# Attention times a gated network in float32: values projected for four heads at once, with fewer buffers

## The chip, the core and the metric

The kernel runs as one launch on one core of a Trainium2 chip. The metric is device time in microseconds (us); lower is better. All inputs and the output are float32 in DRAM.

## The reference

For x of shape [4, 512, 512], with 16 heads of width 128 and an inner width of 1408:

```
xn = layernorm(x)                                   # over the last axis, eps 1e-5
q, k, v = xn W_Q[h] + b_Q[h], xn W_K[h] + b_K[h], xn W_V[h] + b_V[h]
attn = softmax(where(causal, q k^T / sqrt(128), -1e5))
s = sum over h of (attn v) W_O[h] + b_O
f = (silu((xn gate_w^T) gate_s) * ((xn up_w^T) up_s)) down_w^T * down_s
out = x + s * silu(f)
```

## The kernel before

Float32 products go through TensorE as passes of float32r: a tile is held as `hi + lo` (class `Split`), and `mm3` (L90) issues three matmuls for each product, of hi·lo, hi·hi and lo·hi. Making a split costs one copy on ScalarE (`hi`) and one subtraction on VectorE (`lo`); weights are split by ScalarE and GpSimd (`split_w`, L133). The engines work in parallel, each in the order of its own queue, and that order is the order in which the program is written (`manual_schedule`); nothing reorders it.

The attention part is a loop of 64 steps n, over `heads` = (g, b, i): a group g of two heads (HG = 2, so 8 groups), the sequence b (0 to 3), and the head i in the group (0 or 1). A group is 8 steps. One step works on three heads at once:

- `softmax` (L272): scores of this step's head in three PSUM tiles `sc`, four fused mask-and-minimum passes on VectorE (L298), four exponentials on ScalarE (L312), four reciprocals on VectorE (L315), four scalings on GpSimd (L316). It leaves the probabilities in `p`, in one SBUF buffer.
- `turn_p` (L319): turns the probabilities for the value product. Six transposes of 32x32 squares on VectorE write `sq` (L330); a DMA on the queue of SyncE (SP) writes `sq` to DRAM as `turn` (L335); when that has landed, four DMAs on the same queue read `turn` back as `ptr` (L341).
- `split_p` (L346): splits the turned `ptr` of the *previous* step's head into `pt`, two halves, each a ScalarE copy (`pth`, L357) and a VectorE subtraction (`ptl`, L358).
- `project` (L241) makes q and then k of the *next* step's head; their `hi` leaves PSUM on ScalarE (L252), their `lo` on VectorE (L255).
- `attend` (L376), through `attend_last`: the value product z of the previous step's head, from `pt` and the values. It goes key tile by key tile, three passes each.

Two more pieces of work fill the step. In steps with i = 0, `project_v` (L232) makes the values of group g for sequence b, four tiles of 128 tokens by 256 columns (two heads), two before q and two after z. In steps with i = 1, `project_out` (L397) adds the pair of heads of the preceding sequence (`prev`) to the output projection: four tiles, two before q and two after z; each loads its sum so far from DRAM on ScalarE's queue (`load_acc`, L390), adds on VectorE (L406) and stores on SP's queue (L407). `look` (L434) is one VectorE pass per step over a tile of the second part's weights, in steps 9 to 41. Loads of the next group's weights are issued on ScalarE's queue (`prepare_qk`, `prepare_v`, `prepare_o`), and `split_pending` splits them in the step in which they are due.

The order of `split_p` against `turn_p` in a step is set by one flag. With `early` true (steps 2, 3 and the last), the previous head's `split_p` comes after `softmax` and ahead of `turn_p`; in all other steps it comes after `turn_p`, and then two heads' `ptr` are alive at once, for which `ptr` has two buffers:

```
early = n < HG * HG or nxt is None
...
if n > 1 and early:
    pt = split_p(raw)
look()
fill(range(0, half))
if nxt is not None:
    raw_next = turn_p(of)
if not early:
    pt = split_p(raw)
```

The second part, the gated network (`ffn`, L624 on), is not touched by the change but for the name of one constant.

Of the kernel before, what the change touches and what calls it, by code (L numbers as in the profile page):

```python
# [10 lines left out]
F32 = mybir.dt.float32  # L11
# [8 lines left out]
HG = 2  # L20
IGNORE = -100000.0
# [3 lines left out]
LOW_BITS = (1 << 12) - 1  # of a float32's significand, beyond float32r's  # L25


class Split:
    """A float32 tile as hi + lo, each of float32r's 12 significant bits (exact)."""
# [13 lines left out]
def kernel(  # L43
    ctx: ExitStack,
    tc: tile.TileContext,
    x: bass.AP,        # [B, S, D]
    w_q: bass.AP,      # [H, P, ND, E]    w_q[h, p, c, e] = W_Q[h, c*P + p, e]
    w_k: bass.AP,      # [H, P, ND, E]
    w_v: bass.AP,      # [H/HG, P, ND, HG*E]
    w_o: bass.AP,      # [H, E, D]  # L50
    consts: bass.AP,   # [P, 3 H + 2 NF]  b_q, b_k, b_v by head, gate_s, up_s by chunk
    b_o: bass.AP,      # [1, D]
    gate_w: bass.AP,   # [NF, P, ND, P]   gate_w[f, p, c, i] = W[f*P + i, c*P + p]
    up_w: bass.AP,     # [NF, P, ND, P]
    down_w: bass.AP,   # [NF, P, D]       transposed
    down_s: bass.AP,   # [1, D]
    out: bass.AP,      # [B, S, D]
):
    """x + attention(ln(x)) * silu(ffn(ln(x))), in float32.

    A float32 product a*b goes through the tensor engine as three passes of
    float32r: with a = ah + al and b = bh + bl exactly (12 bits each), the passes
    carry ah*bh, ah*bl and al*bh; al*bl is below float32's own rounding.
    """
# [19 lines left out]
    ]  # L84
    acc_d = [
# [4 lines left out]
    def mm3(ps, a, b, first, last):  # L90
        nc.tensor.matmul(ps, a.hi, b.lo, start=first, stop=False)  # L91
        nc.tensor.matmul(ps, a.hi, b.hi, start=False, stop=False)  # L92
        nc.tensor.matmul(ps, a.lo, b.hi, start=False, stop=last)  # L93

# [1 line left out]
    with ExitStack() as at:  # L96
# [6 lines left out]
        vp = at.enter_context(tc.tile_pool(name="vp", bufs=2 * NT))  # L103
# [46 lines left out]
        def split_pending(n):  # L150
            """Split the weights that are due by step n."""
            for due, dst, raw in [p for p in pending if p[0] <= n]:
                split_w(dst, raw)
            pending[:] = [p for p in pending if p[0] > n]

        def prepare(due, dst, src, name):
            """Load a [P, D] piece of a weight; split_pending() splits it when it is due."""
            pending.append((due, dst, stage(src, name)))
# [6 lines left out]
        def prepare_v(g, due):  # L165
            wv[g] = weight(wvop, [P, ND, HG * E], f"wv{g}", "wv")
            half = ND // 2
            for i in range(2):
                c = slice(i * half, (i + 1) * half)
                src = w_v[g][:, c, :].rearrange("p c e -> p (c e)")  # L170
                prepare(due, flat(wv[g][:, c, :]), src, f"wvr{g}_{i}")
# [10 lines left out]
        def ln_stats(b, tt):  # L182
            """Means and variances of some of b's tiles."""
# [14 lines left out]
        def table(func):  # L198
            """Have ScalarE load the function's table now."""
            nc.scalar.activation(small.tile([P, 1], F32, name="junk"), eps, func)  # L200

        def warm_up():
            """Matmuls from the start on, for TensorE's clock."""
# [4 lines left out]
        def ln_normalize(b, t):  # L208
# [4 lines left out]
            xn = lnp.tile([P, D], F32, name="xn")  # L213
            nc.vector.tensor_scalar(xn, xt, mv[:, 0:1], rstd, ALU.subtract, ALU.mult)
            xn_of[b, t] = xn
# [16 lines left out]
        def project_v(g, b, t):  # L232
            ps = ps_mm.tile([P, HG * E], F32, name="psv", tag="mm")
            for c in range(ND):
                mm3(ps, xnT[b][:, c, ts(t, P)], wv[g][:, c, :], c == 0, c == ND - 1)
            v = weight(vp, [P, HG * E], f"v{g}_{b}_{t}", "v")
            nc.scalar.copy(v.hi, ps)
            nc.vector.tensor_tensor(v.lo, ps, v.hi32, ALU.subtract)
            v_of.setdefault((g, b), []).append(v)

        def project(b, h, w, bias, name, parts=1):  # L241
            """q or k of a head, [E, S], by parts; yields before each one leaves PSUM."""
# [18 lines left out]
        # The causal half of the scores is kept by query tile t: [P queries, keys up  # L261
        # to its diagonal], that of the transposed probabilities by key tile j: [P keys,
        # queries from its diagonal on], these in the order [quarter, slot, Q] where
        # slot(j, t) counts the pairs and a query is t * P + quarter * Q + its column.
# [7 lines left out]
        def softmax(qT, kT):  # L272
# [3 lines left out]
            for pack in PACK:  # L276
# [3 lines left out]
                for t in pack:  # L280
                    n = (t + 1) * P
                    where[t] = sc[:, at_ : at_ + n]
                    if t > 0:
                        mm3(where[t], qT[:, ts(t, P)], kT[:, :n], True, True)
                    at_ += n
                if 0 in pack:
                    # so few columns that q.hi's two passes go as one, side by side
# [31 lines left out]
        def turn_p(of):  # L319
            """Transpose the probabilities: squares of Q on VectorE, which DMA puts in place."""  # L320
# [18 lines left out]
            raw = pp.tile([P, NQ, NS * Q], F32, name="ptr", tag="ptr", bufs=2)  # L339
# [21 lines left out]
        def transpose_p(of):  # L361
            """The same on TensorE, in less time."""
# [13 lines left out]
        def attend(h, pt, vs):  # L376
            z = ps_mm.tile([P, NT, P], F32, name="z", tag="mm")
            for j in range(NT):
                c = slice(slot[j], slot[j] + NT - j)
                mm3(z[:, j:, :], vs[j][:, ts(h % HG, E)], pt[:, c, :], j == 0, j == NT - 1)  # L380
            zT = weight(zp, [P, NT, P], f"z{h}", "z")
            # the rows of the probabilities sum to one, so v's bias goes in here
# [14 lines left out]
        def project_out(g, b, t, zTs):  # L397
# [3 lines left out]
            if g == 0:  # L401
                a = ap.tile([P, D], F32, name="a", tag="a")
                nc.vector.tensor_tensor(a, ps, bo_bc, ALU.add)
# [14 lines left out]
        # Are all the ffn's weights float32r already (12 significant bits)?  The  # L418
        # bits of each partition are or-ed together on the way.
# [19 lines left out]
        def low_bits():  # L439
            """By partition, the low 12 bits found; 0 if they are clear in every weight."""  # L440
# [5 lines left out]
        def any_of(low):  # L446
            """Their sum as [1, 1] int32."""
# [6 lines left out]
        with tc.manual_schedule():  # L454
# [4 lines left out]
            prepare_v(0, -2)  # L459
# [45 lines left out]
            bo_bc = load_const(b_o.broadcast_to([P, D]), [P, D], "bo_bc")  # L505
            ds_bc = load_const(down_s.broadcast_to([P, D]), [P, D], "ds_bc")
# [11 lines left out]
            for n, (g, b, i) in enumerate(heads):  # L518
# [4 lines left out]
                # the layernorm of a later b, from its statistics to its transposing  # L523
# [7 lines left out]
                def fill(ks):  # L531
                    for t in ks:
                        if i == 0 and not (n == 0 and t == 0):
                            project_v(g, b, t)
                        if i == HG - 1 and prev is not None:
                            project_out(*prev, t, zs[prev])

                # at the ends there is less to do while the last step's p is turned
                early = n < HG * HG or nxt is None
# [3 lines left out]
                if n > 1 and early:  # L543
                    pt = split_p(raw)
                look()
                half = NT // 2 if nxt is not None else NT - 1
                fill(range(0, half))
                if nxt is not None:
                    raw_next = turn_p(of)
                if not early:  # L550
                    pt = split_p(raw)
                split_pending(n)
                # loads for the steps to come
# [4 lines left out]
                if nxt is None:  # L558
                    # in wv's place, which is done with
# [7 lines left out]
                if g + 1 < NG:  # L567
                    # in place of this group's, when these have had their last use
# [228 lines left out]
```

## Time and profile before

| | |
|---|---|
| runs, median (lowest to highest) | 1237.92 us (1237.6 to 1238.34) |
| profiled execution, first to last instruction (span) | 1235.7 us |
| what lies outside the span | 1.9 to 2.6 us, from the runs |
| granted TensorE clock, mean | 0.998 |
| PE busy | 1208.2 us (98%) |
| DVE / ACT / POOL busy | 828.0 / 526.2 / 302.4 us |
| DMA moved | 215.55 MB, mean 174 GB/s |
| first scores of step 0, and of step 63 | 19.88 and 968.77 us |

How to read it: the page is one profiled execution; PE is TensorE's matmuls, PEld its weight loads, DVE VectorE, ACT ScalarE, POOL GpSimd, SPq and ACTq the DMA queues of SyncE and ScalarE. A matmul's duration includes its way through the array, so that two neighbours overlap: what a matmul costs in a row of them is the distance from its start to the next one's. A line of the timeline has start and duration in us, engine, source line, operation, output and inputs, the count of merged instructions, and in brackets the engine's idle time before it and what ended that. A line of the waits has the total in us, the number of waits and the longest. A DMA row ends with the median time from issue to landing.

### The profile page before, as it was taken

What the parts mean: (1) busy time and instruction counts of PE and PEld (TensorE: products, weight loads), DVE (VectorE), ACT (ScalarE), POOL (GpSimd) and SP (SyncE); (2) the same over time, 40 slices, a digit from 0 to 9 for tenths busy, and PEclk for the clock granted to TensorE, in tenths of its full rate; (3) what the DMA queues carried; (4) which work ended last, traced back from release to release, by engine and by line L of the source; (5) the groups of instructions that cost most, each with busy time, mean ns of one, the idle gap of its engine ahead of it and who ended that gap; (6) DMA issues with size and microseconds to landing.
All of it is one profiled execution on the core that took longest, in us unless ns stands there. A gap on an engine that the chain in (4) does not pass through costs nothing.

```text
span 1235.7 us, 18827 instructions
## 1 busy us (share of the span) xinstructions
PE 1208.2 (98%) x6514; PEld 1049.4 (85%) x6514; DVE 828.0 (67%) x2044; ACT 526.2 (43%) x1169; POOL 302.4 (24%) x433
## 2 busy tenths in 40 slices
PE   8999999999999999999999999999999999999997
PEld 7888888888888888888888888888888888888886
DVE  6897777777777777777777676767676634334343
ACT  5654444444444444444544454445444332323231
POOL 4212321232123212321322141214121341212110
PEclk9999999999999999999999999999999999999999
DMA  4464456656665666566655555566544793637341
GB/s 163 134 191 144 137 167 192 205 171 188 188 205 170 189 203 207 172 199 198 217 176 175 179 173 171 169 188 183 170 163 153 239 331 95 205 94 206 84 145 38
DMA packets 117912, 215.55 MB, mean 174 GB/s; under 512 B 13232, under 2 KB 45744, under 8 KB 117808
## 3 DMA queue, kind: packets, MB, share of 16 engines
q1 hardware_dynamic: 74016, 134.51, 34.2%
q10 hardware_dynamic: 29376, 53.26, 14.4%
q0 software_dynamic: 14416, 26.48, 8.0%
q8 instruction: 53, 0.87, 0.3%
q14 instruction: 51, 0.42, 0.1%
HBM read 135.17 MB, written 79.04 MB: 173 GB/s over the span
## 4 chain that ended last, share of the span: by engine, by line
PE 82%; DVE 11%; ACT 2%; POOL 1%; issue 1%; DMA 1%; SPq 0%; DVEq 0%; ACTq 0%
PE pd L660 6%; PE pg L660 6%; PE pu L660 6%; DVE ptl L358 5%; PE pso L91 5%; PE psv L91 4%; PE pso L93 4%; PE pso L92 4%; PE psv L93 4%; PE psv L92 4%; PE z L91 3%; PE psq L91 3%; PE psq L92 3%; PE psq L93 3%; PE psk L93 3%; PE psk L92 3%
## 5 line engine op out<-in xcount | busy, mean ns | idle before, releaser
L316 POOL TENSOR_SCALAR p<-p,rtot 128x512 f32<-128x512 f32 (+3 forms) x256 | 148.6, 602 | 688.8 <-DVE rtot L315 688.8
L312 ACT ACTIVATE p<-p,nmax 128x512 f32<-128x512 f32 (+3 forms) x256 | 140.9, 552 | 147.1 <-DVE nmax L298 147.1
L358 DVE TENSOR_TENSOR ptl<-ptr,pth 128x640 fp32r<-128x640 f32 x126 | 132.8, 1092 | 1.4 <-ACT pth L357 1.4
L330 DVE STREAM_TRANSPOSE sq<-p 128x256 f32<-128x256 f32 x378 | 113.3, 362 | 0.0
L298 DVE CUSTOM_DVE_ANT_0 p<-sc,mask 128x512 f32<-128x512 f32 (+2 forms) x192 | 96.5, 553 | 0.3 <-PE sc L93 0.3
L252 ACT ACTIVATE k<-psk,consts 128x512 fp32r<-128x512 f32 (+1 forms) x65 | 44.2, 680 | 108.3 <-PE psk L93 108.1
L357 ACT CAST pth<-ptr 128x640 fp32r<-128x640 f32 x126 | 84.9, 724 | 1.5 <-DMA ptr<-turn 1.5
L252 ACT ACTIVATE q<-psq,consts 128x512 fp32r<-128x512 f32 (+1 forms) x65 | 44.3, 682 | 96.8 <-PE psq L93 72.4
L406 DVE TENSOR_TENSOR a<-pso,a 128x512 f32<-128x512 f32 x108 | 72.1, 687 | 17.4 <-PE pso L93 17.4
L255 DVE SCALAR_TENSOR_TENSOR k<-psk,consts,k 128x512 fp32r<-128x512 f32 (+1 forms) x65 | 48.0, 739 | 53.2 <-ACT k L252 53.1
L686 DVE SCALAR_TENSOR_TENSOR hd<-pu,consts,sg 128x512 f32<-128x512 f32 x44 | 33.0, 751 | 66.7 <-PE pu L660 62.2
L315 DVE RECIPROCAL rtot<-tot 128x1 f32<-128x1 f32 x256 | 41.6, 163 | 42.7 <-ACT p L312 36.3
L91 PE MATMUL sc<-k,q 128*128 128x512 f32 (+2 forms) x192 | 65.8, 342 | 1.8 <-DVE xl L225 1.6
L92 PE MATMUL sc<-k,q 128*128 128x512 f32 (+2 forms) x192 | 64.7, 337 | 0.0
L93 PE MATMUL sc<-k,q 128*128 128x512 f32 (+2 forms) x192 | 64.7, 337 | 0.0
L255 DVE SCALAR_TENSOR_TENSOR q<-psq,consts,q 128x512 fp32r<-128x512 f32 (+1 forms) x65 | 47.6, 732 | 7.6 <-ACT q L252 7.6
L312 ACT ACTIVATION_READ_ACCUMULATOR p<-p,nmax 128x1 f32 x256 | 47.7, 186 | 0.0
L91 PEld LDWEIGHTS sc<-k,q 128*128 128x128 f32 x192 | 36.2, 188 | 7.9 <-DVE xl L225 3.6
L716 ACT ACTIVATE o<-o 128x512 f32<-128x512 f32 (+1 forms) x17 | 10.3, 607 | 68.8 <-DVE o L715 68.8
L91 PE MATMUL z<-ptl,v_0h 128*128 128x512 f32 x64 | 27.0, 421 | 12.6 <-DVE ptl L358 12.6
L92 PEld LDWEIGHTS sc<-k,q 128*128 128x128 f32 x192 | 36.2, 188 | 3.6
L93 PEld LDWEIGHTS sc<-k,q 128*128 128x128 f32 x192 | 36.1, 188 | 2.6
(734 smaller groups left out, 3811.2 us busy)
## 6 DMA issues: line engine op xcount, KB each, us to landing
turn<-sq SPq DMA_DIRECT2D x63, 640.0 KB, 3.7
ptr<-turn SPq DMA_DIRECT2D x252, 160.0 KB, 3.4
acc<-a SPq DMA_DIRECT2D x124, 256.0 KB, 3.8
a<-acc ACTq DMA_DIRECT2D x108, 256.0 KB, 2.9
xt<-in_x SPq DMA_DIRECT2D x16, 256.0 KB, 4.2
wor<-in_w_o ACTq DMA_DIRECT2D x16, 256.0 KB, 5.1
fa<-acc SPq DMA_DIRECT2D x16, 256.0 KB, 6.3
fx<-in_x SPq DMA_DIRECT2D x16, 256.0 KB, 6.7
```

Source lines behind the costliest of these rows:

```text
L91: nc.tensor.matmul(ps, a.hi, b.lo, start=first, stop=False)
L92: nc.tensor.matmul(ps, a.hi, b.hi, start=False, stop=False)
L93: nc.tensor.matmul(ps, a.lo, b.hi, start=False, stop=last)
L252: nc.scalar.activation(q.hi[:, at_], ps[:, at_], AF.Identity, bias=bias[:, h : h + 1])
L255: nc.vector.scalar_tensor_tensor(q.lo[:, at_], ps[:, at_], bias[:, h : h + 1], q.hi32[:, at_], ALU.add, ALU.subtract,)
L298: nc.vector.tensor_tensor_reduce(out=of[t], in0=where[t], in1=add, scale=-SCALE, scalar=BIG, op0=ALU.add, op1=ALU.min, accum_out=nmax[t],)
L312: nc.scalar.activation(of[t], of[t], AF.Exp, bias=nmax[t], scale=-1.0, accum_out=tot)
L316: nc.gpsimd.tensor_scalar(of[t], of[t], rtot, 1.0, ALU.mult, ALU.mult)
L330: nc.vector.transpose(dst.rearrange("p a s i -> p s a i"), src.rearrange("p (s a i) -> p s a i", s=n, i=Q),)
L357: nc.scalar.copy(dst(pt.hi), src)
L358: nc.vector.tensor_tensor(dst(pt.lo), src, dst(pt.hi32), ALU.subtract)
L660: nc.tensor.matmul(ps, l, r, start=first and k == 0, stop=last and k == len(pairs) - 1)
```

## The change

- `project_v` computes 512 columns (four heads, VG = 2 groups) at a time, in every second group (g even). The first half of the result is used from SBUF; the second half is written to DRAM (`v_d`, 64 DMAs of 256 KB on SP's queue), and in the odd groups read back by `load_v` (32 DMAs of 512 KB on ScalarE's queue), one sequence ahead.
- The work of a step is spread anew. In even groups a step with i = 0 projects values tile 0 ahead of q and tile 1 after z, a step with i = 1 tiles 2 and 3 ahead of q. In odd groups no values are projected. Of the output projection, two tiles go after z in steps with i = 1, and the other two ahead of q in the step after (i = 0 of the next sequence, `prev2`).
- `split_p` always comes ahead of `turn_p`, as before in steps 2 and 3; `ptr` has one buffer in place of two.
- The layernorm writes in place, the two broadcast constants share a tile (`row_bc`), the value pool has 6 buffers of 512 columns hi and lo in place of 8 of 256. The weights of the values are loaded and split in four pieces of which the last two wait for a staging buffer at the start, and in two steps of an odd group later.
- `mm3` begins with hi·hi; in the scores the pass with k's `lo` comes last. `attend` goes over all key tiles with hi·hi, then with v's `lo`, then with the probabilities' `lo`, in the order 0, 3, 1, 2 of key tiles.

```diff
-        vp = at.enter_context(tc.tile_pool(name="vp", bufs=2 * NT))
+        vp = at.enter_context(tc.tile_pool(name="vp", bufs=NT + 2))
...
         def project_v(g, b, t):
-            ps = ps_mm.tile([P, HG * E], F32, name="psv", tag="mm")
+            ps = ps_mm.tile([P, VG * HG * E], F32, name="psv", tag="mm")
             for c in range(ND):
                 mm3(ps, xnT[b][:, c, ts(t, P)], wv[g][:, c, :], c == 0, c == ND - 1)
-            v = weight(vp, [P, HG * E], f"v{g}_{b}_{t}", "v")
+            both = vp.tile([P, 2, VG * HG * E], F32R, name=f"v{g}_{b}_{t}", tag="v")
+            v = Split(both[:, 0], both[:, 1])
             nc.scalar.copy(v.hi, ps)
             nc.vector.tensor_tensor(v.lo, ps, v.hi32, ALU.subtract)
-            v_of.setdefault((g, b), []).append(v)
+            v_of.setdefault((g, b), []).append(v[:, : HG * E])
+            nc.sync.dma_start(
+                out=v_d[g // VG][b][t // 2, :, t % 2], in_=both.bitcast(F32)[:, :, HG * E :]
+            )
+
+        def load_v(g, b):
+            for k in range(NT // 2):
+                two = vp.tile([P, 2, 2, HG * E], F32R, name=f"v{g}_{b}_{k}", tag="v")
+                nc.scalar.dma_start(out=two.bitcast(F32), in_=v_d[g // VG][b][k])
+                for t in range(2):
+                    v_of.setdefault((g, b), []).append(Split(two[:, t, 0], two[:, t, 1]))
...
-            raw = pp.tile([P, NQ, NS * Q], F32, name="ptr", tag="ptr", bufs=2)
+            raw = pp.tile([P, NQ, NS * Q], F32, name="ptr", tag="ptr")
...
-            for j in range(NT):
-                c = slice(slot[j], slot[j] + NT - j)
-                mm3(z[:, j:, :], vs[j][:, ts(h % HG, E)], pt[:, c, :], j == 0, j == NT - 1)
+            todo = []
+            for part, other in (("hi", "hi"), ("lo", "hi"), ("hi", "lo")):
+                for j in (0, NT - 1, 1, 2):
+                    v = getattr(vs[j], part)[:, ts(h % HG, E)]
+                    p_ = getattr(pt, other)[:, slot[j] : slot[j] + NT - j, :]
+                    todo.append((z[:, j:, :], v, p_))
+            for k, (o, v, p_) in enumerate(todo):
+                nc.tensor.matmul(o, v, p_, start=k == 0, stop=k == len(todo) - 1)
...
-                def fill(ks):
-                    for t in ks:
-                        if i == 0 and not (n == 0 and t == 0):
-                            project_v(g, b, t)
-                        if i == HG - 1 and prev is not None:
+                prev2 = divmod(gb - 2, B) if gb > 1 else None
+                values = g % VG == 0
+
+                def early():
+                    if i == 0:
+                        if prev2 is not None:
+                            for t in range(NT // 2, NT):
+                                project_out(*prev2, t, zs[prev2])
+                        if values and n > 0:
+                            project_v(g, b, 0)
+                    elif values:
+                        project_v(g, b, 2)
+                        project_v(g, b, 3)
+
+                def late():
+                    if i == 0 and values:
+                        project_v(g, b, 1)
+                    if i == HG - 1 and prev is not None:
+                        for t in range(NT // 2):
                             project_out(*prev, t, zs[prev])
...
-                if n > 1 and early:
+                if n > 1:
                     pt = split_p(raw)
                 look()
-                half = NT // 2 if nxt is not None else NT - 1
-                fill(range(0, half))
+                early()
+                if nxt is None:
+                    for t in range(NT - 1):
+                        project_out(*prev, t, zs[prev])
                 if nxt is not None:
                     raw_next = turn_p(of)
-                if not early:
-                    pt = split_p(raw)
                 split_pending(n)
...
+                    if i == HG - 1 and divmod(gb + 1, B)[0] % VG:
+                        load_v(*divmod(gb + 1, B))
+                elif i == HG - 1 and b + 1 < B:
+                    load_v(g, b + 1)
```

## The prediction, made before the changed kernel ran

> **What bounds the kernel now.** I read the page's busy times first, then the waits, then the timelines of TensorE, VectorE, ScalarE and SP's queue over single steps, and at last the DMA rows.
>
> ```profile
> PE 1208.2 (98%) x6514; PEld 1049.4 (85%) x6514; DVE 828.0 (67%) x2044; ACT 526.2 (43%) x1169; POOL 302.4 (24%) x433
> ```
>
> TensorE sets the time: 98% busy, and 27 us idle in all. Of that idle time the waits (PE's own) name one large cause, the `lo` half of the turned probabilities, which comes late to the value product:
>
> ```profile
> PE z L91 <- DVE ptl L358: 12.6, 19, 0.8
> ```
>
> The timeline of PE gives the price of a matmul, as the distance of two starts (columns: start, duration, both us):
>
> ```profile
> 300.21 0.39 PE L93 MATMUL psk<-xh,wk5l 128*128 128x512 f32 x1
> 300.44 0.39 PE L91 MATMUL psk<-xl,wk5h 128*128 128x512 f32 x1
> ...
> 304.08 0.28 PE L92 MATMUL psv<-wv2h,xh 128*128 128x256 f32 x1
> 304.20 0.28 PE L93 MATMUL psv<-wv2h,xl 128*128 128x256 f32 x1
> ```
>
> Over longer rows of them this is 0.2273 us for 512 columns (11 distances from 311.38 to 313.88) and 0.1195 us for 256 (22 from 304.08 to 306.71). So a step's parts on PE are: scores 1.75 (306.83 to 308.58), a tile of the output projection 6 x 0.2273 = 1.36, q and k 12 x 0.2273 = 2.73 each, z 1.98 (301.93 to 303.91), a value tile 12 x 0.1195 = 1.43. A step with i = 0 is then 1.75 + 4 x 1.43 + 5.46 + 1.98 = 14.92, one with i = 1 14.63; the scores of steps 8 and 63 start at 140.28 and 968.77, so that the mean step takes 15.06, 0.28 of it waits.
>
> The changed order of `split_p` and `turn_p` makes a second resource matter, the way of the probabilities through DRAM. Steps 2 and 3 of the kernel before already run in the order that the change gives to all. Step 2, ACT, DVE and SP in turn:
>
> ```profile
> 52.77 1.34 ACT L357 CAST pth<-ptr 128x640 fp32r<-128x640 f32 x2
> ```
> ```profile
> 53.51 1.64 DVE L358 TENSOR_TENSOR ptl<-ptr,pth 128x640 fp32r<-128x640 f32 x2 [0.45 <-ACT pth L357]
> 55.07 0.41 DVE L238 TENSOR_TENSOR v_0l<-psv,v_0h 128x256 fp32r<-128x256 f32 x1
> ...
> 55.74 1.79 DVE L330 STREAM_TRANSPOSE sq<-p 128x256 f32<-128x256 f32 x6
> ```
> ```profile
> 57.56 0.34 SPq L335 DMA_DIRECT2D turn<-sq  x1
> 60.58 1.73 SPq L341 DMA_DIRECT2D ptr<-turn  x4
> ```
>
> The old head's split stands on DVE ahead of the new head's transposes. In the other steps it stands behind them (step 20 of before):
>
> ```profile
> 327.07 1.80 DVE L330 STREAM_TRANSPOSE sq<-p 128x256 f32<-128x256 f32 x6
> 328.80 1.52 DVE L358 TENSOR_TENSOR ptl<-ptr,pth 128x640 fp32r<-128x640 f32 x2
> ```
>
> There a turned head has nearly two steps to come back; nothing waits for it (ScalarE waited for `ptr` 1.5 us in all). The way itself is long:
>
> ```profile
> turn<-sq SPq DMA_DIRECT2D x63, 640.0 KB, 3.7
> ptr<-turn SPq DMA_DIRECT2D x252, 160.0 KB, 3.4
> ```
>
> The four reads are issued over 1.73 us, so with these medians the last has landed 3.7 + 1.3 + 3.4 = 8.4 us after the transposes. Read step by step from the landings, this time (call it L) is 7.8 to 12.4, median 9.1. In groups 1 to 4 it is 9.35 in steps with i = 0 and 10.25 in those with i = 1, where two stores of sums stand just ahead on SP's queue; in groups 5 to 7, without the loads for `look`, 8.4 and 9.7.
>
> **The change part by part.**
>
> *Wider value projection.* 1536 matmuls of 256 columns become 768 of 512: 768 x (2 x 0.1195 - 0.2273) = 9.0 us less on PE, all of it on the path while PE sets the time. The trace's two distances put the cost that a matmul has besides its columns at 11.7 ns. The Trainium skill, page "TensorE: Matmul & The Clock Gate", Part 1 ("Wait — 56ns, not 53.3ns?"), gives a warm matmul only about 2.5 ns beside its columns; by that the saving would be 1.9 us and the time 7 us higher, an estimate from the page, which this trace does not support.
>
> *Reordered value product and scores.* The pass with the probabilities' `lo` goes last, and that `lo` is made earlier in the step, so the 12.6 us of idle go, with the stretched first passes beside them. Matmul count and columns are unchanged; a lone 128-column pass costs its successor 0.06 (308.58 to 308.87 is 0.29 for a 512-column pass), three in a row now cost 0.15 in z: no difference. What is late next on PE is only its own work: with all waits gone 56 steps lose 0.28 x 56 = 16 us.
>
> *Work spread anew.* PE's share of a step becomes 1.75 + 2 x 1.36 + 2 x 2.73 + 5.46 + 1.98 = 17.37 in even groups and 1.75 + 2.72 + 5.46 + 1.98 = 11.91 in odd ones (11.9 for i = 0 and i = 1 alike). Steps 8 to 63 were 56 x 15.06 = 843.4; on PE alone they become 24 x 17.37 + 32 x 11.91 = 798.0, 45.4 less. Group 0 gets dearer, as it does the values of group 1 too: 15 tiles in its loop from 1.43 to 2.73 (+19.5), two tiles of output projection fewer (-2.7), so +16.8.
>
> *Start.* Pieces three and four of the values' weights need staging buffers that GpSimd frees at 8.8 and 10.0 (where the second head's weights are loaded now); they land some 3.4 later, and ScalarE's queue stands at their copies: the third layernorm statistic behind them, at 10.66 now, moves to about 14.2, and the first value tile takes 1.3 more: +4.8, with 1.3 to 7 as bounds.
>
> *Split ahead of turn, one `ptr` buffer.* This is the part that decides. In every step a head's return from DRAM now stands ahead, on DVE, of the next head's transposes, and these ahead of that head's trip. This is a loop that goes round once in a step: landing, split 2.30 (52.77 to 55.07), `look` 0.74 where there is one, for i = 0 two adds 1.20, transposes 1.82 (55.74 to 57.56), then L. Behind the waiting copy `pth` on ACT stand the hi of q and k, for which the next scores wait; so when the loop is longer than PE's 11.91, PE waits. In odd groups with `look` (1 and 3), L for i = 0 is as before for i = 1, since the stores of sums now stand there, 10.25; for i = 1 I take 10.0, between 9.35 and 10.25, as 1 MB of `load_v` takes the place of the stores. Sum: 2.30 + 0.74 + 1.20 + 1.82 + 10.25 = 16.3 and 2.30 + 0.74 + 1.82 + 10.0 = 14.9, mean 15.6. In groups 5 and 7, with L of 9.4 and 9.2 (between 8.4 and 9.7): 14.7 and 13.3, mean 14.0. That is 16 x 15.6 + 16 x 14.0 = 474, and 7 more for the steps in which GpSimd splits weights beside `look` (two-input passes from SBUF take 1600 ns beside it where 797 is the rule) and for two looks in group 5: 481, or 15.0 a step, against 381 on PE: +100. In even groups the loop is 2.30 + 0.74 + 1.20 + 0.65 + 1.82 + 10.5 = 17.2 and 16.3, just under PE's 17.37; I allow +4 in all, 0 to 15.
>
> *DMA.* 64 stores and 32 loads, 33.5 MB more on 215.55: they matter through L alone. *ScalarE and VectorE* save one fixed cost per pair of value tiles (two copies of 0.37 become one of about 0.62), off the path. The in-place layernorm moves the loads of x behind PE's transposes on SP's queue, ahead of a `turn` that comes some us later; the shared constant and the value pool make no wait, since the last readers are a step old: 0, and if that cover failed, a few us once.
>
> The Trainium skill, same page and part, says that an idle window of about 3.4 us halves TensorE's clock until it has been busy for as long. That speaks against steps that leave PE idle for 3 us; the trace of before, with PE's clock at 0.99 to 1.00 in each stretch and no idle stretch over 1.7 us, cannot show it. By the page such a step would cost PE up to 1.7 us, an estimate, and that lies inside the idle time that the loop leaves.
>
> **Sum.** Against the profiled execution of 1235.7 (the runs' median is 2.2 above, and I carry that over): -45.4 + 16.8 + 4.8 + 100 + 4 = +80, so 1316 as a span and 1318 as a time.
>
> **Rivals.** (a) *PE stays the bound in odd groups too.* For it: the matmuls do become fewer, and all of PE's waits have a remedy here. Then only -45.4 + 16.8 + 4.8 = -24 remains: 1214. The point from which it decides: an odd step below 11.91 + 24/32 = 12.65 us makes the change a gain. That needs L near 7.2 on the mean, below the 7.8 that is the smallest of 63 in the trace. (b) *The loop holds, but light:* L at its quiet 7.8 to 8.4 throughout, since even groups move other data: odd steps of 12.7 to 13.5, 1240 to 1265. (c) *L grows with the added transfers* to the 12 of the slowest steps: odd steps of 17, and the even groups above PE by half a us a step: 1375 to 1390. (d) That the narrow matmuls were not the cost, and the 9.0 us do not come: 1327, inside the forecast.
>
> **How the numbers follow.** The forecast, loop-bound odd groups at 13.5 to 16.6 a step, has 0.80 (1265 to 1370); (a) 0.06; (b) 0.07, of which a quarter ends within 0.2% of before; (c) 0.07. The range runs from 1262 to 1375. A measurement of this kernel tells about 0.2% (2.5 us) from no change: faster 0.06, same 0.02, slower 0.92.
>
> **What would show it.** Right: odd groups' steps near 15, even ones near 17.4; ACT `pth` waiting for the DMA of `ptr` for some 3 us in nearly each odd step (before: 1.5 us in all), PE's idle time near 120 us, its wait for `ptl` in z gone, and 768 value matmuls 0.227 apart. Wrong: steps under 12.65 in odd groups, `pth` not waiting, or PE idle in even groups.

## The result, and the profile after

| | before | after |
|---|---|---|
| runs, median (lowest to highest) | 1238.13 us (1237.6 to 1239.83) | 1326.61 us (1324.91 to 1327.73) |
| profiled execution: span | 1235.7 us | 1325.3 us |
| first scores of step 0 | 19.88 us | 24.63 us |
| granted TensorE clock, mean | 0.998 | 0.97 |
| DMA moved | 215.55 MB | 249.01 MB |

The changed kernel is slower: 1.0711 times the time of before, with a 95% interval of 1.0696 to 1.0727. That lies 9 us above the 1318 that was forecast, and inside the range.

The busy times of the page after, its row of the granted clock, and the engines' shares of the chain that ended last:

```profile
PE 1239.3 (94%) x5746; PEld 1031.8 (78%) x5746; DVE 786.8 (59%) x1980; ACT 519.6 (39%) x1105; POOL 297.7 (22%) x433
...
PEclk8999998899999988999999989999999999999999
...
PE 56%; DMA 19%; DVE 14%; ACT 4%; SPq 3%; issue 3%; POOL 1%; ACTq 0%; DVEq 0%; POOLq 0%
```

There are 768 matmuls fewer, and yet TensorE is busy for longer than before, at 94% of a longer span. In the clock's row the 8s behind the first stand in three places, which are the odd groups 1, 3 and 5 (a slice is 33.1 us; group 1 is about 164 to 288). The chain that ends last is TensorE's work for little more than half; DMA, VectorE and the two queues hold most of the rest. Both the waits and the DMA rows say where:

```profile
DVE ptl L383 <- ACT pth L382: 177.9, 62, 7.8
ACT pth L382 <- DMA ptr<-turn: 144.8, 41, 7.3
...
PE z L412 <- ACT pth L382: 33.7, 27, 3.3
...
PE sc L98 <- ACT k L277: 22.6, 7, 3.8
```
```profile
turn<-sq SPq DMA_DIRECT2D x63, 640.0 KB, 4.6
ptr<-turn SPq DMA_DIRECT2D x252, 160.0 KB, 3.3
```

TensorE's 12.6 us of waiting for `ptl` in z are gone. In their place ScalarE's copy `pth` waits for the turned probabilities 41 times, 3.5 us each; before it did so for 1.5 us in all. TensorE then waits for that copy in z, and for k (which stands behind the copy on ScalarE) in the scores.

A cut through four groups shows the two kinds of step (columns: stretch, length, busy time and count of PE, PEld, DVE, ACT and POOL, clock, DMA share, GB/s). These are about groups 1 to 4:

```profile
164.00:288.00 124.00, 105.48 (x472) 86.93 (x472) 78.21 (x211) 50.17 (x114) 31.65 (x42) 0.92 0.65 203
288.00:428.00 140.00, 139.84 (x667) 117.99 (x666) 92.11 (x237) 57.39 (x126) 28.25 (x39) 1.00 0.66 206
428.00:554.00 126.00, 106.97 (x474) 87.64 (x473) 78.89 (x213) 50.25 (x114) 31.66 (x42) 0.91 0.68 208
554.00:694.00 140.00, 139.84 (x667) 117.96 (x666) 92.27 (x236) 57.15 (x126) 30.16 (x38) 1.00 0.64 204
```

In even groups TensorE has no gap: 139.84 of 140, at 17.4 us a step. In odd groups it has 18.5 to 19 us of gaps in eight steps, a lower clock, and no other engine is busy for more than two thirds of the time. Nothing is at its limit there, so the limit is a chain through several engines. It can be walked in step 28 (group 3), with ACT first, then SP, DVE and PE:

```profile
493.00 0.19 ACT L337 ACTIVATION_READ_ACCUMULATOR p<-p,nmax 128x1 f32 x1
499.42 0.72 ACT L382 CAST pth<-ptr 128x640 fp32r<-128x640 f32 x1 [6.24 <-DMA ptr<-turn]
...
505.60 0.69 ACT L277 ACTIVATE q<-psq,consts 128x512 fp32r<-128x512 f32 x1 [3.77 <-issue]
```
```profile
494.41 1.73 SPq L366 DMA_DIRECT2D ptr<-turn  x4
...
506.36 0.32 SPq L360 DMA_DIRECT2D turn<-sq  x1
510.85 1.74 SPq L366 DMA_DIRECT2D ptr<-turn  x4
```
```profile
500.18 1.56 DVE L383 TENSOR_TENSOR ptl<-ptr,pth 128x640 fp32r<-128x640 f32 x2 [6.80 <-ACT pth L382]
501.66 1.76 DVE L469 TENSOR_TENSOR bits<-bits,look 128x512 int32<-128x512 int32 x1
503.34 1.27 DVE L438 TENSOR_TENSOR a<-pso,a 128x512 f32<-128x512 f32 x2
504.54 1.79 DVE L355 STREAM_TRANSPOSE sq<-p 128x256 f32<-128x256 f32 x6
```
```profile
506.92 0.80 PE L98 MATMUL sc<-k,q 128*128 128x512 f32 x1 [2.79 <-ACT k L277]
```

ScalarE has finished the exponentials at 493.2 and stands still until the head of the step before has landed. The four reads were issued at 494.41; the copy starts at 499.42, 5.0 us later. Then VectorE does the `lo` half, the pass for `look`, two adds and at last the transposes of the next head, and only at 506.36 can that head's trip begin. Its reads are issued 4.5 us later, and the next round has started. From 494.41 to 510.85 it is 16.4 us, where TensorE's own work for such a step is 11.9.

Not every wait in this step is on the loop. Between the copy and q, ScalarE stands for 3.77 us at its own load issues, two of which wait for GpSimd to free a staging buffer, and the scores' wait of 2.79 us comes from that. It costs nothing here: the next step's exponentials are done at 512.0 all the same, and the copy behind them waits until 515.95 for its DMA.

### The profile page after: what moved, and what is told of

The parts are those of the page before. It is cut to its first block, busy times and chain, and to the rows that moved or that the text cites. A ratio compares the mean times of both kernels' runs of the same rounds, so it can differ in the third digit from the quotient of the medians.

```text
span 1325.3 us, 17330 instructions
## 1 busy us (share of the span) xinstructions
PE 1239.3 (94%) x5746; PEld 1031.8 (78%) x5746; DVE 786.8 (59%) x1980; ACT 519.6 (39%) x1105; POOL 297.7 (22%) x433
## 2 busy tenths in 40 slices
DMA packets 141970, 249.01 MB, mean 188 GB/s; under 512 B 14768, under 2 KB 67760, under 8 KB 141872
## 4 chain that ended last, share of the span: by engine, by line
PE 56%; DMA 19%; DVE 14%; ACT 4%; SPq 3%; issue 3%; POOL 1%; ACTq 0%; DVEq 0%; POOLq 0%
DMA turn<-sq 9%; DMA ptr<-turn 9%; PE psv L103 8%; PE pd L712 6%; PE pg L712 6%; PE pu L712 6%; PE z L412 4%; DVE sq L355 4%; PE psv L98 4%; PE pso L103 4%; PE psk L103 4%; PE psq L103 4%; DVE ptl L383 3%; PE sc L103 3%; SPq L366 3%
## 5 line engine op out<-in xcount | busy, mean ns | idle before, releaser
L341 POOL TENSOR_SCALAR p<-p,rtot 128x512 f32<-128x512 f32 (+3 forms) x256 | 154.5, 622 | 696.4 <-DVE rtot L340 696.4
L383 DVE TENSOR_TENSOR ptl<-ptr,pth 128x640 fp32r<-128x640 f32 x126 | 99.2, 827 | 177.9 <-ACT pth L382 177.9
L382 ACT CAST pth<-ptr 128x640 fp32r<-128x640 f32 x126 | 85.1, 724 | 145.1 <-DMA ptr<-turn 144.8
L412 PE MATMUL z<-pth,v 128*128 128x512 f32 (+3 forms) x512 | 98.7, 337 | 33.7 <-ACT pth L382 33.7
L412 PEld LDWEIGHTS z<-pth,v 128*128 128x128 f32 x512 | 81.8, 195 | 54.3 <-ACT pth L382 45.5
L103 PE MATMUL sc<-k,q 128*128 128x512 f32 (+2 forms) x384 | 109.8, 371 | 12.1 <-DVE q L280 10.6
L98 PE MATMUL sc<-k,q 128*128 128x512 f32 (+2 forms) x192 | 71.8, 374 | 25.3 <-ACT k L277 22.6
L103 PEld LDWEIGHTS sc<-k,q 128*128 128x128 f32 x384 | 74.0, 207 | 27.2 <-DVE q L280 13.8
L253 DVE TENSOR_TENSOR v<-psv,v 128x512 fp32r<-128x512 f32 x64 | 43.7, 685 | 39.5 <-ACT v L252 39.2
L98 PEld LDWEIGHTS sc<-k,q 128*128 128x128 f32 x192 | 39.7, 207 | 33.2 <-ACT k L277 25.2
L252 ACT CAST v<-psv 128x512 fp32r<-128x512 f32 x64 | 37.3, 583 | 71.2 <-PE psv L103 71.2
L280 DVE SCALAR_TENSOR_TENSOR q<-psq,consts,q 128x512 fp32r<-128x512 f32 (+1 forms) x65 | 46.6, 717 | 14.6 <-ACT q L277 14.5
L412 PE MATMUL z<-ptl,v 128*128 128x512 f32 (+3 forms) x256 | 54.0, 335 | 0.0
## 6 DMA issues: line engine op xcount, KB each, us to landing
v<-v ACTq DMA_DIRECT2D x32, 512.0 KB, 6.9
```

Of the source, the lines that this page charges most:

```text
L98: nc.tensor.matmul(ps, a.hi, b.hi, start=first, stop=False)
L103: nc.tensor.matmul(ps, l, r, start=False, stop=last and k == 1)
L280: nc.vector.scalar_tensor_tensor(q.lo[:, at_], ps[:, at_], bias[:, h : h + 1], q.hi32[:, at_], ALU.add, ALU.subtract,)
L341: nc.gpsimd.tensor_scalar(of[t], of[t], rtot, 1.0, ALU.mult, ALU.mult)
L382: nc.scalar.copy(dst(pt.hi), src)
L383: nc.vector.tensor_tensor(dst(pt.lo), src, dst(pt.hi32), ALU.subtract)
```

## Experiments

The kernel before was run beside each (medians 1238.07 to 1238.82). Here is the whole set; a step is the mean one of odd groups.

| run | time, us | ratio (95%) | odd step, us | `pth` waits, us (times) |
|---|---|---|---|---|
| after | 1326.61 | 1.0711 (1.0696 to 1.0727) | 15.2 | 144.8 (41) |
| e1_two_ptr | 1326.33 | 1.0709 (1.0688 to 1.0731) | 15.1 | 140.5 (42) |
| e2_late_split | 1283.47 | 1.0370 (1.0335 to 1.0404) | 13.9 | 49.7 (24) |
| e3_early_in_before | 1223.43 | 0.9878 (0.9861 to 0.9894) | 14.8 | 5.6 (8) |
| e4_more_pe | 1330.29 | 1.0741 (1.0709 to 1.0774) | 15.3 | 98.4 (35) |
| e5_no_v_traffic | 1279.00 | 1.0325 (1.0302 to 1.0348) | 13.7 | 77.7 (35) |
| e6_late_look_pool | 1265.37 | 1.0220 (1.0171 to 1.0269) | 13.4 | 66.1 (27) |
| e7_order_in_before | 1222.49 | 0.9869 (0.9853 to 0.9886) | 14.8 | 0.9 (2) |
| e8_early_and_order | 1224.22 | 0.9886 (0.9870 to 0.9903) | 14.8 | 5.2 (8) |
| e9_late_no_traffic | 1231.96 | 0.9944 (0.9921 to 0.9966) | 12.4 | 25.3 (19) |
| e10_light_steps | 1188.58 | 0.9593 (0.9565 to 0.9621) | 13.6 (groups 4 to 7) | 106.9 (40) |

### Is it the buffer? (e1_two_ptr)

The changed kernel with two buffers for `ptr`. For the room, the sums of the output projection use a pool of two, and two of the four tiles borrow the buffers of the layernorm's input.

```diff
-            raw = pp.tile([P, NQ, NS * Q], F32, name="ptr", tag="ptr")
+            raw = pp.tile([P, NQ, NS * Q], F32, name="ptr", tag="ptr", bufs=2)
```

> The changed kernel with two buffers for ptr in place of one; the order of split_p ahead of turn_p stays. (For room, two of the four tiles of sums loaded from DRAM are taken from the layernorm's pool.) Theory, the loop is made by the order of the two on VectorE's queue: no change, 1320 to 1333 us, odd groups' steps at 15.2 to 15.6, pth still waiting some 145 us in all for the DMA of ptr. Rival, the single buffer holds the reads of the next head back: odd steps fall towards PE's 11.9 to 12.6, 1215 to 1240 us.

Measured: 1326.33, the same as the changed kernel, and the same wait:

```profile
ACT pth L382 <- DMA ptr<-turn: 140.5, 42, 7.3
```

So the single buffer costs nothing. With the split ahead of the turn, one buffer is all that this order can use.

### Is it the order of split and turn? (e2_late_split, e3_early_in_before)

First, e1 with the old order from step 4 on:

```diff
-                if n > 1:
+                early_split = n < HG * HG or nxt is None
+                if n > 1 and early_split:
                     pt = split_p(raw)
...
                     raw_next = turn_p(of)
+                if not early_split:
+                    pt = split_p(raw)
```

> As e1_two_ptr, and split_p goes back behind turn_p from step 4 on, as in the kernel before; wide values, their way through DRAM, the spread over two steps and the order of the products stay. Theory, the loop: it no longer goes round once a step, so odd groups come down to what PE and VectorE need, 12 to 13 us a step, and the whole to 1220 to 1250 us, with hardly a wait of pth for ptr. Rivals, the transfers of the values or TensorE's halved clock or the uneven spread: most of the loss stays, 1290 us or more.

Measured: 1283.47 (four runs, 1279 to 1288), 43 us less than with the changed order, but above the expected range. A part of the wait remains, and a new one has come. In step 25, ACT, then SP:

```profile
442.29 1.26 ACTq L262 DMA_DIRECT2D v<-v  x2
452.14 0.34 ACTq L464 DMA_DIRECT2D look<-in_down_w  x1
452.58 0.69 ACT L277 ACTIVATE q<-psq,consts 128x512 fp32r<-128x512 f32 x1 [10.84 <-DMA ptr<-turn]
```
```profile
442.14 0.34 SPq L360 DMA_DIRECT2D turn<-sq  x1
448.76 2.21 SPq L366 DMA_DIRECT2D ptr<-turn  x4
```

ScalarE issues a load for `look`, which needs nothing from the probabilities, only 8.6 us after the loads ahead of it, when the reads of `ptr` that SP issued at 448.76 have come in. In the trace's records the DMAs issued by SP and by ScalarE share eight semaphores, and in none of 806 pairs does a DMA start before the one ahead of it on its semaphore has landed. The issue for `look` has five long waits of this kind in this run, 3.7 to 9.4 us each, 38.7 us in all, each of them for a `turn` or `ptr` of SP (the expectation of e6 below says 15 waits and 39 us; the sum holds, the count does not). In the changed kernel no such wait for `look` shows, which fits that ScalarE has there waited for the same landing in `pth` already. The copies of q and k stand behind that issue on ScalarE.

Then the reverse: the kernel before, with the split always ahead of the turn.

```diff
-                early = n < HG * HG or nxt is None
+                early = True
```

> The kernel before with split_p ahead of turn_p in all steps (early true); nothing else. Theory, the loop, with the parts of the prediction: in groups 1 to 4 2.3 + 0.8 + 0.8 + 1.8 + 9.35 = 15.0 for i = 0 and 2.3 + 0.8 + 1.2 + 1.8 + 10.25 = 16.4 for i = 1, mean 15.7 against 15.1 now; in groups 5 to 7 14.2, under PE's 14.8: 1240 to 1262 us, with pth waiting for ptr in groups 1 to 4. Rival, the order alone does no harm and only takes the wait of z for ptl away: 1222 to 1237 us.

Measured: 1223.43, 1.2% faster than before, and each of the groups 1 to 6 takes 118.19 us, or 14.77 a step, which is TensorE's own work. The expected 1240 to 1262 was wrong, and for an instructive reason. The sum behind it took the trip's time L from before (9.35 on the mean of all steps); with the early split it measures 8.36. The DMA row of this run shows which leg is shorter:

```profile
turn<-sq SPq DMA_DIRECT2D x63, 640.0 KB, 2.9
```

The write lands in 2.9 us where it took 3.7. With the early split, `turn` is issued later in the step, 9.7 us after the first scores in place of 7.6 (groups 1 to 5), when other loads and stores of the step are further along; that this is the reason was not tried by itself. The loop without its slack is then 13.4 to 14.6 us in groups 1 to 5, just under TensorE's 14.77. The order that the change makes universal is thus no loss where steps are even at 14.8 us. It is a loss where TensorE has only 11.9 us of work.

### Is TensorE the bound in odd groups? (e4_more_pe)

The changed kernel with 12 more matmuls of 512 columns in each step of the odd groups but the last, behind the split and ahead of z, with a result that is not used: 2.73 us a step.

```diff
+                if nxt is not None and g % VG:
+                    junk = ps_mm.tile([P, S], F32, name="junkmm", tag="mm")
+                    for k in range(12):
+                        c = k % ND
+                        nc.tensor.matmul(junk, wk[nh].hi[:, c, :], xnT[b].hi[:, c, :],
+                                         start=k == 0, stop=k == 11)
```

> The changed kernel with 12 more matmuls of 512 columns, into a PSUM tile that nobody reads, ahead of z in every step of the odd groups: 2.73 us more for PE in each of 32 steps, 87 us in all. Theory, the loop through DRAM sets odd steps and PE stands idle for 3 us in each: 1315 to 1340 us, PE's idle time down by 60 us or more, its clock in the odd groups back near 1.0. Rival, TensorE (its work or its clock) sets the odd steps: 1390 to 1415 us if its work does; if the halved clock is what costs, the busier PE gains, 1290 to 1310 us.

Measured: 1330.29, from two runs of 1327.05 and 1333.53, so that the 4 us above the changed kernel are not clear of noise. Some 85 us of added matmuls (372 of them, at 0.2273) are hidden but for that. The busy times, and group 1 in the same stretch as above:

```profile
PE 1294.6 (98%) x6118; PEld 1085.2 (82%) x6118; DVE 790.5 (60%) x1980; ACT 518.9 (39%) x1105; POOL 307.6 (23%) x433
```
```profile
164.00:288.00 124.00, 119.40 (x569) 99.21 (x568) 78.84 (x212) 49.86 (x114) 33.05 (x42) 1.00 0.64 203
```

TensorE's idle time falls by 55 us, from 86.0 to 30.7, a little less than expected. The group still takes 124 us. The last line also answers the question about the clock: it is 1.00 here and 0.92 in the changed kernel. The 97 added matmuls are 22.0 us, so the other 472 took 97.4 at the full clock against 105.48: the low clock lengthened TensorE's work by 8.1 us in this group, and all of that lay inside the waits, since filling them gave the clock back and no time.

### How much is the added traffic? (e5_no_v_traffic)

The changed kernel with only the first four stores of values and one load.

```diff
-            nc.sync.dma_start(
-                out=v_d[g // VG][b][t // 2, :, t % 2], in_=both.bitcast(F32)[:, :, HG * E :]
-            )
+            if g == 0 and b == 0:
+                nc.sync.dma_start(
+                    out=v_d[g // VG][b][t // 2, :, t % 2], in_=both.bitcast(F32)[:, :, HG * E :]
+                )
...
         def load_v(g, b):
+            if fixed:
+                v_of[g, b] = fixed
+                return
...
```

> The changed kernel without the values' way through DRAM: of the 64 stores and 32 loads only the first four stores and one load are left, and all odd groups use those values (wrong ones; matmuls, waits on them aside, are the same). Theory, the loop: in odd groups the 1 MB of load_v that stands ahead of turn in steps with i = 1 goes, so turn lands in about 4 us there in place of 6.2, i = 1 steps lose some 2.2 us, 16 of them 35 us: 1280 to 1305 us, odd steps still near 14.5, above PE's 11.9. Rival, the added transfers are the cause: 1215 to 1250 us. Rival, they are hidden: 1320 us or more.

Measured: 1279.0 (two runs, 1276.85 and 1281.15), 47 us less than e1, which has the same pool for the sums, and 1 us below the expected range. The write's row, which had 4.6 us:

```profile
turn<-sq SPq DMA_DIRECT2D x63, 640.0 KB, 3.1
```

In odd groups' steps with i = 1, where the 1 MB of `load_v` stood ahead of `turn`, the time from the issue of `turn` to that of the reads falls from between 6.1 and 6.7 us to between 3.1 and 3.6. From the reads' issue to the last landing it is 5.0 to 5.3 us in both kernels. So the traffic acts through this one leg of the trip. It is the loads that cost: the even groups, in which the stores are issued, take 139.2 to 139.7 us with and without them.

### Both causes away (e6_late_look_pool, e9_late_no_traffic)

e6 is e2 with the loads for `look` issued by GpSimd, so that ScalarE no longer stands behind them.

```diff
-                nc.scalar.dma_start(out=raw, in_=src)
+                nc.gpsimd.dma_start(out=raw, in_=src)
```

> e2_late_split with the loads for look issued on GpSimd's queue in place of ScalarE's. In e2 the issue of such a load on ScalarE's queue waited 15 times, 39 us in all, for the semaphore that it shares with an earlier DMA of the other queue (SP and ACT share eight), and ScalarE's copies of q and k stood behind it. Theory, that wait is what e2 had left: 1235 to 1255 us, odd groups at 12 to 13.5 a step. Rival, the added transfers of the values hold the odd steps in any order: 1275 us or more.

Measured: 1265.37, 18 us less than e2, but 10 above the expected range: ScalarE's new wait was not all that was left. (Its four runs lie between 1261 and 1274, further apart than those of the other kernels.) With the transfers of the values in flight the trip is 10.8 to 13.6 us here in groups 1, 3 and 5, so even in the old order it does not always fit into steps of 11.9.

e9 is e6 with e5's edit as well, and a value pool of five buffers.

> e6_late_look_pool and e5_no_v_traffic together: the changed kernel with split_p behind turn_p from step 4 on, the loads for look on GpSimd's queue, and the values' way through DRAM left out but for its first part (odd groups use wrong values; value pool of 5 buffers). Each alone left odd steps at 13.3 and 14.0 us. Theory, what is left in each is the trip of the probabilities, too long in e5 since the loop goes round in one step and in e6 since the other transfers lengthen it: together odd steps come to 12 to 12.6 us, PE's own, 1220 to 1240 us. Rival, the uneven spread costs something more than the trip (VectorE, the halved clock): odd steps stay at 13 us or more, 1250 us or more.

Measured: 1231.96, as expected. Odd steps take 12.4 us, even ones 17.39, and the clock is back at 0.995. The four corners of the two causes:

| | values through DRAM | not through DRAM |
|---|---|---|
| split ahead of turn | 1326.33 (e1) | 1279.00 (e5) |
| split behind turn, `look` on GpSimd | 1265.37 (e6) | 1231.96 (e9) |

The order, with `look` moved to GpSimd, is worth 61 us with the traffic and 47 without it; the traffic 47 with the early split and 33 with the late one. Together they are 94 us, and 88 are the difference of the changed kernel to the one before. The order alone is e2's 43 us; the early split with `look` on GpSimd was not run.

### What the other parts are worth (e7_order_in_before, e8_early_and_order)

e7 is the kernel before with the new order of passes in `mm3`, the scores and `attend`, and nothing else.

```diff
-        nc.tensor.matmul(ps, a.hi, b.lo, start=first, stop=False)
-        nc.tensor.matmul(ps, a.hi, b.hi, start=False, stop=False)
-        nc.tensor.matmul(ps, a.lo, b.hi, start=False, stop=last)
+        nc.tensor.matmul(ps, a.hi, b.hi, start=first, stop=False)
+        passes = [(a.hi, b.lo), (a.lo, b.hi)]
+        if b_last:
+            passes.reverse()
+        for k, (l, r) in enumerate(passes):
+            nc.tensor.matmul(ps, l, r, start=False, stop=last and k == 1)
...
+            for part, other in (("hi", "hi"), ("lo", "hi"), ("hi", "lo")):
+                for j in (0, NT - 1, 1, 2):
```

> The kernel before with the order of passes of the changed one (mm3 from hi hi on, the scores' pass with k's lo last, the value product by passes and key tiles 0, 3, 1, 2); split_p stays late. Theory of the prediction: z no longer waits for ptl, which was 12.6 us of idle and some 3 of stretched passes: 1221 to 1229 us. Rival, the wait only moves to pth or to the scores: 1236 to 1240 us.

Measured: 1222.49, 1.3% faster than before, and the lowest time here but for e10, which does less work. Its page:

```profile
PE 1204.6 (99%) x6514; PEld 1049.9 (86%) x6514; DVE 826.4 (68%) x2044; ACT 525.4 (43%) x1169; POOL 301.8 (25%) x433
...
PE 95%; DVE 3%; ACT 1%; issue 0%; DMA 0%; SPq 0%; ACTq 0%
```

The wait for `ptl` in z no longer stands among TensorE's waits, of which the longest kinds are now 1.9 us in all. e8 has the early split in addition.

> e3_early_in_before with the order of passes of the changed kernel. e3 is at PE's own 14.77 us a step with no wait left, so theory says no difference to e3: 1220 to 1225 us. Rival, the order of passes costs or gains by itself: 3 us or more off e3's 1223.4.

Measured: 1224.22, no further gain: two remedies for the same 16 us.

### Does a light step alone make the loop the bound? (e10_light_steps)

e8, without the wide values and without any of their traffic, with less work for TensorE in groups 4 to 7 (11.98 us a step).

```diff
                     for t in ks:
+                        if g >= NG // 2 and t >= NT // 2 and nxt is not None:
+                            if i == 0:
+                                v_of[g, b].append(v_of[g, b][t - NT // 2])
+                            continue
```

> e8_early_and_order (balanced steps, split_p ahead of turn_p, 14.77 us a step, all of it PE's) with PE's work after z left out in groups 4 to 7: two of four value tiles (the first two are used twice) and two of four tiles of the output projection, with their stores. PE's share of these 31 steps falls from 14.77 to 11.98 us. Theory, the loop: it lies just below 14.77 and does not get shorter, but for some lighter traffic: these steps stop at 13.3 to 14.4 us, and the whole at 1180 to 1212 us, with pth waiting for ptr in most of them. Rival, PE sets them: 1133 to 1142 us.

Measured: 1188.58, and steps of 13.6 us in groups 4 to 7. The wait comes back in a kernel where it had been 5.2 us:

```profile
ACT pth L360 <- DMA ptr<-turn: 106.9, 40, 4.5
```

So the loop has a floor of its own, some 13.6 us where no values pass through DRAM, and TensorE's share of a step shows only above it.

## Why the prediction was right, and where its sizes were off

**Mechanism.** The likeliest case was that odd groups are bound by the loop of landing, split, transposes and trip. `pth` waiting some 3 us in nearly each odd step (measured: in all 32 of them, 4.1 us on the mean; the other 9 of its 41 waits are in even groups), even steps near 17.4 (17.44), odd ones near 15 (15.21) and the end of the wait for `ptl`: all are in the trace. e1, e4, e9 and e10 then show it by taking parts away: not the buffer, not TensorE, but order and traffic on steps too light to cover the loop.

**The sum.** The span grew by 89.6 us, forecast 80:

| term | predicted | measured |
|---|---|---|
| start, to the first scores | +4.8 | +4.8 |
| group 0 | +16.8 | +19.2 |
| steps 8 to 62 | +58.6 (to step 63) | +61.6 |
| from step 63's scores to the end | 0 | +4.0 |

The 58.6 are the text's -45.4 + 100 + 4. That the first row agrees is in part luck. ScalarE's queue and the longer value tile give 2.4 and 1.3 us of it; another 1.1 comes from matmuls that ran at half the clock from 16.9 to 20.3, which the prediction did not have.

The same thing is a part of what the sum missed in group 0 and at the end, where TensorE sets the time and nothing hides it. In step 3 of group 0 the clock is at half for one stretch of 3.4 us. The first two lines are the changed kernel, before and in that stretch; the third is the same work in e9, where the clock stayed up:

```profile
71.50:74.90 3.40, 1.84 (x9) 1.04 (x9) 3.40 (x6) 0.59 (x1) 0.00 (x0) 1.00 1.00 225
74.90:78.30 3.40, 3.40 (x12) 2.82 (x11) 2.69 (x14) 2.51 (x9) 1.07 (x2) 0.50 0.96 336
```
```profile
74.00:77.40 3.40, 3.40 (x18) 2.89 (x18) 2.71 (x14) 2.35 (x9) 0.91 (x2) 1.00 0.83 287
```

12 matmuls fall into this stretch in place of 18, and the step took 21.16 us against 19.59 in e9: 1.6 of the 2.4 us by which group 0 exceeds its term. The last row, which the prediction had not looked at, has 1.6 us from step 63's scores, at half the clock again (3.38 us for 1.75), and 1.4 from z, which waits longer for `pth`, as the loop goes round once more at the end (`pth` waits 3.0 us in that step).

**The loop's terms.** Groups 1 and 3, where they were worked out singly:

| term, us | predicted i = 0 / 1 | measured i = 0 / 1 |
|---|---|---|
| split | 2.30 | 2.32 |
| `look` and adds | 1.94 / 0.74 | 2.46 / 0.80 |
| transposes | 1.82 | 1.82 |
| L, issue of `turn` to last landing | 10.25 / 10.0 | 8.89 / 11.14 |
| start of the copy after the landing | 0 | 0.1 |
| sum | 16.3 / 14.9 | 15.6 / 16.2 |

The sum of the two is 31.8 against 31.2 (two such steps took 31.1 us in group 1 and 31.5 in group 3), but L was mis-sized both ways, and the errors cancel: that the mean came out is luck. In steps with i = 1 the 1 MB of `load_v` costs the trip more than the two stores of sums that it was put level with; in steps with i = 0, with the stores ahead of it, the trip was shorter than the one with stores before, for a reason that was not traced. The adds and `look` measure more because in six of the eight steps with i = 0 `look` runs beside GpSimd's split of a weight (1.76 to 1.79 us for 0.68 otherwise); the prediction had that as an allowance. (Its 1600 ns against 797 for such a pass stand in no row; `ptl` in the trace of before has a median of 811 and up to 1919.) For groups 5 and 7 the mean of 14.0 was too low: group 5 took 15.2 a step and group 7 14.2, for the same reason in L (11.3 and 11.7 for i = 1, against 9.2). The even groups' allowance of 4 us came to under 2.

**TensorE's own savings.** The value matmuls stand as the trace of before had priced them:

```profile
293.70 0.39 PE L98 MATMUL psv<-wv2h,xh 128*128 128x512 f32 x1
293.93 0.39 PE L103 MATMUL psv<-wv2l,xh 128*128 128x512 f32 x1
```

Twelve of them go from 293.70 to 296.42, 0.2267 apart, so the 9.0 us were real work removed, and rival (d) falls, though its 1327 is the time that was measured. All value tiles stand in even groups, where TensorE sets the time, so that this saving counts. The 16 us of the reordered passes are real as well: e7 has them alone (1238.8 to 1222.5).

The Trainium skill's 2.5 ns beside a warm matmul's columns ("TensorE: Matmul & The Clock Gate", Part 1) stays at odds with this kernel, where two distances give 11.7 ns; the measurement decides. The same part's rule on idle windows agrees with the trace in the length and not in the idleness. The clock record of the changed kernel has half-clock stretches of 3.4 us, or two or three times that. But ahead of most of them TensorE was idle for only a part of 3.4 us: for 1.56 us ahead of the one in step 3 (3.40 less the 1.84 busy, in the lines under "The sum"), for 2.2 us ahead of the one at 201.2. With waits of about 3 us in the odd steps the mean clock is 0.91 to 0.92 in groups 1 and 3, and with e4's filling it is 1.00 in group 1. The prediction's judgement that the price lies inside the loop's idle time is what e4 shows for the odd groups; in the start, group 0 and the end, some 4 us in all, it does not hold.

**Idle time.** TensorE's idle time is 86 us (1325.3 - 1239.3), not near 120. The low clock hides the rest, as matmuls that it stretches count as busy. An estimate from e4: its 84.6 us of added matmuls raise the busy time by only 55.3 (1294.6 - 1239.3), so some 29 us of the changed kernel's busy time were stretch, which would make 115.

**Rivals.** (a), TensorE as the bound, needed odd steps under 12.65; e9 reaches 12.4 by taking both causes away, and is indeed below the time of before, by 0.6%. (b) did not come: no quiet L with the transfers in flight. (c) had its L in half of the steps, but the even groups stayed with TensorE.

**What the reasoning had wrong.** It treated L as a property of the step. e3 shows that it changes with the point at which `turn` is issued, and e5 with what is in flight at that moment. For the change itself the error was small; for e3 it turned a gain of 15 us into a forecast loss.

## What to carry to other kernels

When work is concentrated in some steps, check the light steps against each chain that goes round once in a step, with its DMA legs: an engine that is 98% busy on the average sets the time only in steps that are longer than that chain. Before making a transfer's consumer come ahead of the next transfer, add up the whole round trip and price its DMA legs by what will be in flight at the moment of the new issue, not by the old median. And where several parts of a change each have a reason, run the cheapest alone: here the order of the passes gave 1.3%, and the changed kernel takes 8.5% longer than that one.

## What was not expected of the hardware

- An issue of a DMA on ScalarE's queue can wait for a DMA that SP issued, as the two share eight semaphores in this program: in e2 the loads for `look` waited 38.7 us in five issues, 8.6 us in the one shown, and ScalarE's computing stood behind them.
- A 640 KB write to DRAM took 2.9 us in the median in e3 and 4.6 in the changed kernel: the same transfer, issued at another point of the step and beside other transfers.
- A clock of 0.91 to 0.92 in groups 1 and 3 cost nothing: e4 brought it back to 1.00 in group 1 with added matmuls, and the group took as long. Where TensorE sets the time it does cost: 1.6 us for a single stretch of 3.4 us in step 3, ahead of which TensorE had been idle for less than half of as long a stretch.

It stays open whether the wide projection pays if its work is spread evenly over even and odd groups, so that each step has 14.6 us for TensorE. That was not tried; it may need a second set of the values' weights to be held at once.
